# Layer 1 of a four-layer graph network: source blocks in groups of three instead of two, with VectorE's blocks at the second place of each three

## The chip, the core and the metric

The kernel runs on one core of a Trainium2 chip. The metric is device time in microseconds (us), the median of several executions. The core has five engines with a queue of their own each: TensorE (PE in the profile; its weight loads are PEld), VectorE (DVE), ScalarE (ACT), GpSimd (POOL) and SyncE (SP), which issues the DMA transfers. An engine takes its instructions in order; one that waits holds up all behind it on that engine.

## The reference, cut to what matters

Four graph layers follow each other on a dense 3327 x 3327 adjacency matrix and 64 features per node. Each ends with a residual sum and a layer norm. The change lies in layer 1:

```python
c = CURV
deg = jnp.maximum(adj.sum(axis=1, keepdims=True), 1e-08)
w = adj / deg
log_ij = _logmap(x[:, None, :], x[None, :, :], c)
agg = jnp.einsum('ij,ijc->ic', w, log_ij)
transformed = agg @ weight + bias
return _expmap(origin, transformed, c)
```

For each pair of nodes a factor that depends on the inner product of their features is multiplied with the adjacency, and the result weights a sum over the source nodes.

## The kernel before, in words

Nodes are padded to 3328: 26 blocks of 128. Destinations are taken in 4 chunks of 832 columns (two halves of 416), in the order 0, 3, 1, 2. In layer 1 (`layer1_far`, line 822) a step i is one source block of one chunk; there are 4 x 26 = 104 steps. The adjacency comes in pairs of source blocks, 832 KB each, into four buffers (`adjp`).

Each step has these parts:

- **Row products**, `far_v`, line 835: two products of 64 rows x 128 columns (one for each half), fp32, each recorded as two matmuls, so four records a block. Their result, tile `two`, takes a pair of PSUM banks; there are three such pairs, given out in rotation by `Banks.pair` (line 305). In this text V7 is the row product of step 7.
- **First factor**, line 846: VectorE reads `two` and the adjacency and writes `p` (four buffers).
- **Second factor.** A step marked "G" in `L1_ENGINES`: ScalarE squares `two` into `s` (line 859), adds a constant (line 860), and GpSimd multiplies `s` by `p` (line 861). A step marked "V": ScalarE squares `two` in place (line 851) and VectorE makes `s` from `two` and `p` (line 854, the function `last`). So `two` of a G step is free after the square, that of a V step only after line 854. The last four steps are V whatever the pattern says (`L1_LAST`).
- **Sums**, `far_aggregate`, line 866: two products of 128 rows x 64 columns with `s`, again four records a block, six steps later (`L1_AHEAD`). A7 is the sum of step 7; the accumulators are `one0` and `one1`.

The loop at line 936 takes a group of steps: first the row products of all of them, then the factors step by step, then the sums of as many steps. Within the factors, line 854 of step i-1 is issued behind the `p` of step i. TensorE's order is held by manual dependencies: row products behind the last sum of the group before (`summed`), sums behind the group's row products (`v_issued`).

```python
for start in range(0, total + L1_AHEAD, L1_GROUP):
    group = range(start, start + L1_GROUP)
    ...
    for i in group:
        ...
            v, v_issued = far_v(c, jb, summed)
    ...
    for i in group:
        ...
            s, next_last, p_issued = far_factors(v, a, engine)
        ...
        if last is not None:
            issued = last()
        ...
    for i in group:
        ...
            summed = far_aggregate(*waiting.pop(0), acc, j == 0, j == NB - 1, v_issued)
```

Other work is threaded in by step number, on the same engines: the last chunk's features from layer 0 (`features0`, line 605, from step 3 on), their transposes (`transposes0`, line 650, with copies at 656 and 657) at two steps that stand two apart, and, for every finished chunk, the copies and the product of its sums (`keep1`, lines 451 and 880), the products `own1` (line 889), and `epilogue1` with `finish1` (lines 895 and 798: products at line 903, then some 30 small VectorE operations at 910 to 923 and 804 to 820). The products of line 903 go into `pv`, which `Banks.short` takes out of the same three pairs of banks: the next one in rotation.

Of the kernel before, what the change touches and what calls it, by code (L numbers as in the profile page):

```python
# [79 lines left out]
L0_LAG = 3  # L80


L1_ENGINES = "GVGGGV"
L1_AHEAD = 6

L1_LAST = 4

L1_GROUP = 2

# [27 lines left out]
def four_gnn_layers_kernel(  # L119
# [702 lines left out]
    def layer1_far(banks):  # L822
        with tc.tile_pool(name="l1w", bufs=1) as wp:
# [19 lines left out]
            def far_factors(v, a, engine):  # L843

                p = tile_p()
                issued = nc.vector.scalar_tensor_tensor(  # L846
                    halves(p), v, 0.25 - 0.5 * FD, halves(a), op0=ALU.add, op1=ALU.mult
                )
                s = tile_s()
                if engine == "V":  # L850
                    nc.scalar.activation(v, v, AF.Square, bias=FB - 0.5, scale=-2.0)  # L851

                    def last():
                        return nc.vector.scalar_tensor_tensor(  # L854
                            halves(s), v, FG, halves(p), op0=ALU.add, op1=ALU.mult
                        )

                    return s, last, issued
                nc.scalar.activation(halves(s), v, AF.Square, bias=FB - 0.5, scale=-2.0)  # L859
                nc.scalar.activation(s, s, AF.Copy, bias=FG)  # L860
                nc.gpsimd.tensor_mul(s, s, p)  # L861
                return s, None, issued
# [72 lines left out]
            waiting, last, side, total, summed, kept = [], None, None, NCH * NB, None, {}  # L935
            for start in range(0, total + L1_AHEAD, L1_GROUP):
                group = range(start, start + L1_GROUP)
                made = []
# [11 lines left out]
                for i in group:  # L950
                    p_issued, next_last = None, None
                    if made:
                        k, jb, v, a = made.pop(0)
                        assert k == i
                        engine = L1_ENGINES[i % len(L1_ENGINES)] if i < total - L1_LAST else "V"
                        s, next_last, p_issued = far_factors(v, a, engine)
# [566 lines left out]
```

## Time and profile before

| what | us |
|---|---|
| median of 3 executions (520.52 to 521.48) | 521.14 |
| the profiled execution | 522.02 |
| its span, first to last instruction | 520.3 |
| layer 1, from the first row product to the last sum | 154.4 to 343.4 |
| PE busy over the span | 480.4 (92%) |
| DVE, ACT, POOL busy over the span | 386.2, 328.6, 179.5 |
| PE, DVE, ACT, POOL busy within 200 to 240 | 38.87, 33.37, 33.37, 31.04 |
| mean granted TensorE clock | 0.991 |

A duration is that of one instruction; a bracket behind a row tells how long its engine had stood idle and who released it. Matmul ends are modelled; starts are recorded, so distances between starts are what counts on TensorE.

### The profile page before, as it was taken

Reading aid. Unit: us, or ns where it says so; the run is one execution under the profiler, and the core shown is the slowest. Engines: PE = TensorE matmul, PEld = TensorE weight load, DVE = VectorE, ACT = ScalarE, POOL = GpSimd, SP = SyncE. Lnnn points to the kernel's source line nnn. Section 1 sums busy time; section 2 is a strip of 40 time slices with the busy share of each in tenths; the row PEclk is TensorE's granted clock in tenths of the full one; section 3 lists DMA queues with packets and bytes.
Section 4 is the critical chain, followed back from the end, with each engine's and each line's share of the span. In section 5 each row is a group of like instructions: output and inputs, shape, how many; then the busy total and the mean of one; then the engine's idle time right before and its main releaser. Section 6 shows DMA issues by size and latency. Waiting matters only on the chain. (4 is left out here: it accounts for less than half of the span.)

```text
span 520.3 us, 8496 instructions
## 1 busy us (share of the span) xinstructions
PE 480.4 (92%) x3256; PEld 240.1 (46%) x3256; DVE 386.2 (74%) x703; ACT 328.6 (63%) x395; POOL 179.5 (35%) x150
## 2 busy tenths in 40 slices
PE   5999998999967999999999899899999999999993
PEld 3554443454432333433443344354565655556662
DVE  3565438989669978789789978978689766727744
ACT  1435544776878899868977896720277943338941
POOL 2000201203018788867877695600312012200000
PEclk9999999999999999999999999989999999999997
DMA  8999999989529687767866787499869889950002
GB/s 272 321 361 345 356 395 387 332 273 322 197 85 366 224 258 274 253 198 231 289 213 205 256 260 251 148 342 370 278 214 370 289 279 367 344 188 1 1 18 56
DMA packets 46212, 132.52 MB, mean 255 GB/s; under 512 B 6967, under 2 KB 7071, under 8 KB 46099
## 3 DMA queue, kind: packets, MB, share of 16 engines
q1 hardware_dynamic: 45634, 131.35, 73.2%
q0 software_dynamic: 384, 0.52, 0.4%
q8 instruction: 27, 0.44, 0.3%
q14 instruction: 23, 0.18, 0.1%
q10 hardware_dynamic: 144, 0.03, 0.0%
HBM read 130.86 MB, written 0.85 MB: 253 GB/s over the span
## 5 line engine op out<-in xcount | busy, mean ns | idle before, releaser
L861 POOL TENSOR_TENSOR s<-s,p 128x832 f32<-128x832 f32 x67 | 130.1, 1956 | 42.0 <-ACT s L860 26.6
L846 DVE SCALAR_TENSOR_TENSOR p<-two,adj 128x832 f32<-128x832 f32 x100 | 101.2, 1019 | 18.2 <-issue 12.9
L835 PE MATMUL two<-uw 64*128 64x416 f32 x416 | 88.5, 537 | 12.9 <-DVE s L854 6.0
L549 ACT ACTIVATE rank<-two,last_bias 128x832 uint8<-128x832 f32 x78 | 71.7, 952 | 44.8 <-PE two L539 22.9
L467 PE MATMUL one<-adj,x0w 128*64 128x416 f32 x416 | 82.5, 524 | 3.7 <-DMA adj<-in_adjt_dram 2.2
L866 PE MATMUL one<-s,xu 128*64 128x416 f32 x416 | 85.2, 524 | 0.0
L859 ACT ACTIVATE s<-two 128x832 f32<-128x832 f32 x67 | 57.6, 860 | 27.2 <-DVE p L846 24.6
L525 DVE SCALAR_TENSOR_TENSOR mask<-two,minus_last,mask 32x832 bf16<-32x832 f32 x48 | 52.5, 1093 | 29.7 <-PE two L539 26.0
L835 PEld LDWEIGHTS two<-uw 64*128 64x128 f32 x416 | 37.3, 185 | 64.1 <-PE one L866 20.7
L493 DVE TENSOR_SCALAR mask<-adj 128x1664 bf16<-128x1664 f32 x48 | 51.3, 1068 | 15.8 <-DMA adj<-in_adjt_dram 15.2
L1333 PE MATMUL two<-bits,parts 128*64 128x416 bf16 x624 | 62.3, 340 | 0.0
L860 ACT ACTIVATE s<-s 128x832 f32<-128x832 f32 x67 | 60.1, 897 | 1.9
L539 PE MATMUL two<-mask,tri 128*64 128x416 bf16 x416 | 52.6, 342 | 8.7 <-DVE mask L525 6.2
L467 PE MATMUL one<-adj,xr 128*64 128x416 f32 x264 | 57.0, 514 | 0.2 <-DMA adj<-in_adjt_dram 0.2
L1333 PEld LDWEIGHTS <-parts 128*64 128x64 bf16 x624 | 36.9, 110 | 24.1 <-issue 7.3
L866 PEld LDWEIGHTS one<-s,xu 128*64 128x64 f32 x416 | 25.9, 136 | 47.5 <-issue 46.5
L467 PEld LDWEIGHTS one<-adj,x0w 128*64 128x64 f32 x416 | 29.3, 138 | 35.7 <-issue 23.6
L539 PEld LDWEIGHTS <-tri 128*64 128x64 bf16 x416 | 25.6, 110 | 41.3 <-issue 23.2
L1303 ACT ACTIVATE bits<-rank 128x1664 uint16<-128x1664 uint8 x22 | 33.6, 1580 | 14.5 <-PE two L1333 14.1
L854 DVE SCALAR_TENSOR_TENSOR s<-two,p 128x832 f32<-128x832 f32 x37 | 37.5, 1015 | 1.3 <-ACT two L851 1.3
L851 ACT ACTIVATE two<-two 128x832 f32<-128x832 f32 x37 | 31.3, 847 | 5.6 <-DVE p L846 4.8
L549 ACT ACTIVATE uw<-two,last_bias 128x832 uint8<-128x832 f32 x26 | 24.2, 950 | 12.5 <-DVE mask L525 6.4
(270 smaller groups left out, 472.3 us busy)
## 6 DMA issues: line engine op xcount, KB each, us to landing
adj<-in_adjt_dram SPq DMA_DIRECT2D x135, 832.0 KB, 5.3
uw<-in_adjt_dram SPq DMA_DIRECT2D x7, 832.0 KB, 7.3
a<-in_adjt_dram SPq DMA_DIRECT2D x8, 416.0 KB, 6.2
sums<-in_adjt_dram SPq DMA_DIRECT2D x2, 832.0 KB, 6.0
p<-in_adjt_dram SPq DMA_DIRECT2D x4, 416.0 KB, 5.3
s<-in_adjt_dram SPq DMA_DIRECT2D x4, 416.0 KB, 7.6
uw<-in_xt_dram SPq DMA_DIRECT2D x1, 640.0 KB, 10.8
out_dram<-o SPq DMA_DIRECT2D x3, 192.0 KB, 2.5
```

The lines of the kernel that those rows point to most:

```text
L467: issued = nc.tensor.matmul(acc[h * D : (h + 1) * D, 0:HC], lhsT=x[:, 2 * jp + k, 0:D], rhs=a[:, bass.ts(h, HC)], start=(first and k == 1) ...
L493: issued = nc.vector.tensor_scalar(mask, a2, 0.0, None, op0=ALU.not_equal)
L525: ranks.carried = nc.vector.scalar_tensor_tensor(halves(last), ranks.after[P - 32 : P, :, 0:HC], minus_last[P - 32 : P, :], halves(last), ...
L539: issued = nc.tensor.matmul(counts[k][rows, h, 0:HC], lhsT=lhsT[:, rows], rhs=mask[:, of, bass.ts(h, HC)], start=lhsT is tri, stop=(k == 1 ...
L549: ranks.made = nc.scalar.activation(halves(ranks.rank[:, 2 * jp + k, :]), counts[k][:, :, 0:HC], AF.Relu, bias=last_bias,)
L835: issued = nc.tensor.matmul(v[:, h, 0:HC], lhsT=wt[rows, bass.ts(jb, P)], rhs=ut[rows, bass.ds(c * CH + h * HC, HC)], start=True, stop=True,)
L846: issued = nc.vector.scalar_tensor_tensor(halves(p), v, 0.25 - 0.5 * FD, halves(a), op0=ALU.add, op1=ALU.mult)
L859: nc.scalar.activation(halves(s), v, AF.Square, bias=FB - 0.5, scale=-2.0)
L860: nc.scalar.activation(s, s, AF.Copy, bias=FG)
L861: nc.gpsimd.tensor_mul(s, s, p)
L866: issued = nc.tensor.matmul(acc[h * D : (h + 1) * D, 0:HC], lhsT=xu[:, jb, 0:D], rhs=s[:, bass.ts(h, HC)], start=first, stop=last,)
L1333: issued = nc.tensor.matmul(acc3[c][h * D : (h + 1) * D, 0:HC], lhsT=parts[:, 2 * jp + b, bass.ts(part, D)], rhs=bits[:, b, bass.ts(h, HC) ...
```

## The change

Two constants of layer 1's loop differ.

```diff
-L1_ENGINES = "GVGGGV"
+L1_ENGINES = "GVGGVG"
 L1_AHEAD = 6
 
 L1_LAST = 4
 
-L1_GROUP = 2
+L1_GROUP = 3
```

TensorE now runs three blocks' row products and then three blocks' sums. In each group of three the second step is the V step; before, V steps stood at places 1 and 5 of every six, always the second of a pair. The number of V steps stays 37 and that of G steps 67. The three pairs of banks for `two`, the four buffers of `p` and the nine of `s` are as they were. Nothing outside layer 1 is changed.

In the built order, a typical group reads on TensorE: row products of steps i, i+1, i+2, sums of i-6, i-5, i-4; on VectorE: `p` of i, i+1, i+2, then line 854 of i+1; on ScalarE: square and constant of i, square of i+1, square and constant of i+2. The two batches of transposes (4 and 3 of them), which had two groups of their own, stand in one group, and the second waits for ScalarE's copy of the first. SyncE's order of transfers is the same.

## The prediction

> **What bounds the kernel now.** First the page's chain by line, and layer 1's waits: which engine sets its pace.
>
> ```profile
> PE 34%; DVE 6%; DMA 1%; issue 0%; ACT 0%; POOL 0%; ACTq 0%
> ```
>
> ```profile
> ACT s L859 <- DVE p L846: 24.6, 31, 3.0
> ...
> PE two L835 <- DVE s L854: 6.0, 13, 0.9
> ```
> (The second block's columns: who waited for whom, us in total, times, longest.)
>
> I read it as: TensorE carries the end, and within layer 1 it is held up, once it runs, mainly where VectorE's line 854 gives a pair of banks back late. The first row says that ScalarE's square starts behind VectorE's `p` of the same block, though both only read `two`.
>
> Next TensorE's own timeline in an undisturbed stretch (start, us, engine, line, ..., records).
>
> ```profile
> 200.19 1.67 PE L835 MATMUL two<-uw 64*128 64x416 f32 x8
> 201.79 1.62 PE L866 MATMUL one<-s,xu 128*64 128x416 f32 x8
> 203.34 1.67 PE L835 MATMUL two<-uw 64*128 64x416 f32 x8
> 204.93 1.62 PE L866 MATMUL one<-s,xu 128*64 128x416 f32 x8
> ```
>
> A phase of two blocks' row products takes 1.60 us to the start of the sums, the sums 1.55 to the next row products: 3.15 for two blocks. In narrow windows the pairs of records inside a phase start 0.35 apart (202.19, 202.54, 202.89). Four pairs are 1.40, so the two changes of form cost 0.20 and 0.15, **0.35 a group**. Nine groups from 181.18 to 209.74 took 28.56, 3.173 each: almost that floor.
>
> Last, how a block's banks come free, in the full timeline:
>
> ```profile
> 204.41 1.02 DVE L846 SCALAR_TENSOR_TENSOR p<-two,adj 128x832 f32<-128x832 f32 x1 [1.20 <-issue]
> 204.45 0.85 ACT L851 ACTIVATE two<-two 128x832 f32<-128x832 f32 x1
> 205.35 1.01 DVE L854 SCALAR_TENSOR_TENSOR s<-two,p 128x832 f32<-128x832 f32 x1
> 205.47 0.86 ACT L859 ACTIVATE s<-two 128x832 f32<-128x832 f32 x1 [0.17 <-DVE p L846]
> 206.28 1.02 DVE L846 SCALAR_TENSOR_TENSOR p<-two,adj 128x832 f32<-128x832 f32 x1
> 206.36 0.90 ACT L860 ACTIVATE s<-s 128x832 f32<-128x832 f32 x1
> ```
>
> ```profile
> 228.56 1.01 DVE L854 SCALAR_TENSOR_TENSOR s<-two,p 128x832 f32<-128x832 f32 x1
> 229.72 1.67 PE L835 MATMUL two<-uw 64*128 64x416 f32 x8 [0.42 <-DVE s L854]
> ```
>
> Steps between starts: row product to `p` 1.07 (203.34 to 204.41); `p` to its square 1.06 (204.41 to 205.47); square to constant 0.89 (205.47 to 206.36); constant to the next square 0.80 (203.65 to 204.45); in-place square to line 854 0.87 (207.69 to 208.56); line 854 to a `p` behind it 0.93; line 854 to the row product that waited for its banks 1.16 (228.56 to 229.72).
>
> **The change, part by part.**
>
> *Fewer changes of form.* 104 blocks are 52 groups before and 35 after: 17 x 0.35 = 6.0 us less. The floor of a group of three is 12 x 0.35 + 0.35 = 4.55, against 4.73 for three blocks before. This is a saving only where TensorE does not wait.
>
> *All three pairs of banks are taken at once.* Before, a V block's banks were wanted again two groups later: it stands second in its group, its successor first two groups on, 6.30 - 0.78 = 5.5 us after its own start (0.78 is the distance to a group's second block: 200.19 to 200.97). Line 854 stands there behind the next group's first `p`, at 3.15 + 1.07 + 0.93 = 5.15, and the banks are back at 6.31: just in time, hence the 13 short waits. After, its successor is the second of the very next group. Follow one group from the start of its first row product (0): `p` 1.07, square 2.13, constant 3.02, in-place square of the second block 3.82 (its `p` has ended by 3.1, so ScalarE's order decides), line 854 at 4.69, the next group's second row product at **5.85**. TensorE would be there at 4.55 + 0.78 = 5.33. So the change adds a wait of up to 0.52. Behind the waiting instruction stand, on TensorE, the second and third row products and three sums, nothing else can be drawn ahead.
>
> The wait is not paid in full in each group, since the next group's first row product was issued ahead of it and starts the next chain early. From a second row product that waited to the next group's first are 3.85 (0.35 x 10 + 0.35). First to second to first again: 5.85 + 3.85 = 9.70 for two groups, **4.85 a group**, 0.30 over the floor. The other banks don't bind: the first block's are free at 2.13 + 0.86 = 2.99, the third's at about 5.6, wanted at 6.0. VectorE needs 4 x 0.94 = 3.8 and ScalarE 4.2 of the 4.85; GpSimd 3.9.
>
> 35 x 0.30 = 10.5 us added, 6.0 removed: **+4.5 us**. Against the measured 3.173 of two blocks the quiet groups alone lose 4.85 - 4.76 = 0.09 each.
>
> Bounds of the 0.30: below, nothing, if the square could run beside `p` or VectorE is ahead; above 0.52, if the first row product is never early. I take 0.30, as every step in it has a row above.
>
> A rule that speaks for the change, and one against: the Trainium skill, TensorEngine Tiling (Array Packing), section Key Properties, says that a change of tiling mode drains TensorE; the rows' 0.35 agree, and by that alone it would be 6.0 us faster. The same page, PSUM Bottleneck, says that tiling doesn't speed up the emptying of PSUM, which may become the limit; by that the 6.0 would not come at all. The trace has both, so I follow the chain of rows.
>
> *Disturbed groups.* Here I walked the built order of each engine with the steps above. Small VectorE operations cost 0.2 (0.07 alone between big ones), wide ones 0.45 to 0.5.
>
> - Start. Steps 3 to 14 carry layer 0's last features on VectorE. The page's stall there now is the fill (157.64 to 164.71). After, three groups of row products stand ahead of the first sum. Both walks are level when 12 blocks and 6 sums are done (173.8 before, 173.7 after). Then V13 waits for line 854 of step 10, which stands behind five small and two wide operations: 176.45 instead of 174.5. The second batch of transposes, now in the same group as the first, waits about 0.9 for the copy of line 657. Before had 15 blocks and 9 sums at about 179.6, after at 182.5: +2.9, of which 0.6 is in the plain sum: **+2.3**.
> - First epilogue (steps 36 to 60): `pv` of line 903 takes the banks of the group's first block and is read until line 916, which stands behind the next group's first `p`. From V36: V39 6.85, `p` 7.92, line 916 at 9.73, V40 only at 10.45, V42 at 12.5, V43 at 15.45 (it waits for line 854 of V40's block), and further V48 23.85, V54 35.25, V60 45.7. Before: 213.68 to 256.76, 43.1. +2.6, of which 1.0 is in the plain sum: **+1.6**.
> - Second epilogue (63 to 87): here line 910 stands ahead of line 854, and `pv` is read in time. 43.3 against 42.9 before, +0.4; copies of 0.5 each on ScalarE 0.4 more: +0.8, **-0.2** against the plain sum. VectorE's extra work stalls TensorE in both versions.
> - Where products of lines 889 and 903 lie between row products and sums (up to 0.92 and 1.5), the chain runs beside them and the 0.30 is hidden: steps 60 to 63 **-1.2**, steps 84 to the last sum **-2.2** (from V90 30.7 against 31.5).
>
> The five last bold numbers make +0.3; with +4.5 it is **+4.8**. The last 8 sums and what follows are as long as before (6.6 us from the last row product on), so nothing is given back behind layer 1.
>
> *Places of V steps.* V at each second place instead of one and five of six: GpSimd gets two G blocks in 4.85 and never three in a row. Its four waits of VectorE (`p` for a free buffer) are 3.8 us in all, one of them in the fill; the gain lies between 0 and 3.8. I take 0: TensorE's own waits name line 854 and the square, not `p`'s buffers. Transfers: a pair lands in 5.3 us (median) and is asked for some 11 us ahead; three blocks at once cost nothing as long as that holds, and up to one landing, 5.3, if not. I take 0.
>
> From the profiled execution, 522.0, this gives 526.8; the profiled one lies 0.9 above the median, so against the median of 521.1: **525.9 us**.
>
> **Rivals.**
>
> *TensorE sets the pace (faster).* One mechanism: if the way from the first row product to the next group's second is 5.33 or less instead of 5.85, no banks are waited for and 6.0 is gained: 515.1. For it: 92% busy TensorE, and only 6.0 us of waits on line 854 now. Against: six rows in series, all measured, would have to lose 0.52. It decides from 5.33 downward; from 5.85 to about 5.4 gain and loss cancel.
>
> *They cancel.* Half the waits are hidden by own products and epilogues: 521 within 0.2% (1.0 us), which is about what a measurement can tell from no change.
>
> *The full wait in each group.* The first row product isn't early either, since VectorE's side work delays its `p`: 35 x 0.52 = 18.2 - 6.0 = +12.2, 533.3. For it: three epilogues and the start cover some 65 of 104 steps, and VectorE is there nearly full (19.27 of 20 us from 280 to 300). Against: in the walk each second such group is without a wait.
>
> *The order isn't what the diff says.* In three groups the second row product is put behind half of the third, or behind sums; that touches 3 of 35 groups, at most 1 us, and is in the walk.
>
> **How the numbers follow.** The forecast (522.2 to 530): 0.59, 525.9. TensorE's pace (514 to 520.1): 0.19, 515.1. Cancelled: 0.12, 521. Full wait (530 to 534): 0.10, 533.3. So faster 0.19, same 0.12, slower 0.69. The range from 517 leaves out about half of the faster case, and to 532 half of the full wait: 517 to 532.
>
> **What would show it.** Row products of a group starting 4.55 and 5.1 apart in turn, or 4.85 each, in quiet stretches; a row "two L835 <- DVE s L854" of some 10 us or more instead of 6.0; line 854 at 4.7 behind its group's start; a gap ahead of V40 near line 916; the transposes' second batch waiting for line 657. It is wrong if groups start 4.55 apart without waits on line 854, if the square starts ahead of the end of its block's `p`, or if VectorE waits for transfers.

## The result and the profile after

The changed kernel is slower: 528.25 us (525.62 to 529.92, six executions) against 521.44 (520.52 to 524.3, six), a ratio of 1.0119 with an interval of 1.0082 to 1.0155; the medians differ by +6.8 us. The forecast was 525.9, in a range of 517 to 532. The profiled execution of the changed kernel took 529.92 (span 528.1), that of the kernel before 522.02 (span 520.3).

First the page's chain by engine and by line, of the kernel after.

```profile
PE 56%; DVE 25%; ACT 8%; DMA 4%; issue 3%; POOL 0%; DVEq 0%; ACTq 0%
PE one L467 16%; PE two L1333 10%; PE two L835 8%; DVE p L846 7%; PE one L866 7%; PE two L539 5%; DVE mask L525 5%; DMA adj<-in_adjt_dram 4%; PE two L467 3%; DVE s L854 3%; DVE mask L493 3%; ACT s L859 2%; ACT rank L549 2%; ACT s L860 2%; ACT two L851 1%
```

The chain of before adds up to 41% only, so the shares aren't compared; what counts is the second row. Row products (835), `p` (846), the square (859), the constant (860), the in-place square (851) and line 854 are all on it: the six steps of which the prediction built its 5.85 us.

Layer 1's waits in the kernel after (who for whom, us in total, times, longest):

```profile
ACT s L859 <- DVE p L846: 32.2, 33, 3.2
...
PE two L835 <- DVE s L854: 6.6, 9, 2.2
```

The second row was to be "some 10 us or more" and is 6.6, barely above the 6.0 of before. Read alone it would deny the mechanism. TensorE's timeline in a quiet stretch, steps 21 to 29, shows otherwise (start, us, line, records, bracket: idle time and releaser):

```profile
197.34 2.39 PE L835 MATMUL two<-uw 64*128 64x416 f32 x12
...
201.90 0.97 PE L835 MATMUL two<-uw 64*128 64x416 f32 x4
203.23 1.67 PE L835 MATMUL two<-uw 64*128 64x416 f32 x8 [0.36 <-DVE s L854]
...
207.08 2.39 PE L835 MATMUL two<-uw 64*128 64x416 f32 x12
```

Groups start 4.56 and 5.18 apart in turn, and in the second kind the second row product stands off from the first (x4, then x8) and names line 854. That wait stands in every other group only; in the rest TensorE is on time, because the group before was held. And line 854 itself, in the full timeline of the same groups:

```profile
200.38 0.90 ACT L860 ACTIVATE s<-s 128x832 f32<-128x832 f32 x1
201.18 0.85 ACT L851 ACTIVATE two<-two 128x832 f32<-128x832 f32 x1
202.06 1.02 DVE L854 SCALAR_TENSOR_TENSOR s<-two,p 128x832 f32<-128x832 f32 x1 [0.75 <-ACT two L851]
```

It starts 4.72 behind its group's first row product at 197.34 (forecast 4.69), and 203.23 - 202.06 = 1.17 later the banks are back.

Where the time of layer 1 went, from the starts of the row products on TensorE (us; V60 is the row product of step 60; "forecast" is the prediction's own working for the stretch, with the 0.13 a group of its plain sum; the last stretch is what is left of its +4.8):

| stretch | before | after | loss | forecast |
|---|---|---|---|---|
| V0 to V18, layer 0's last features | 29.90 | 35.30 | **+5.4** | +2.9 (to V15) |
| V18 to V36, undisturbed | 29.35 | 30.27 | +0.9 | +0.9 (from V15) |
| V36 to V60, first epilogue | 43.08 | 45.30 | +2.2 | +2.6 |
| V60 to the last sum's start | 86.16 | 84.61 | -1.6 | -1.6 |
| layer 1 | 188.49 | 195.48 | +7.0 | +4.8 |

In the profiled pair the first row product comes 2.4 later, at the end of layer 0, whose code is the same, and what follows layer 1 is 1.6 shorter; so the spans differ by 7.8.

The start is the one stretch that misses clearly. TensorE there, in the kernel after:

```profile
177.13 0.97 PE L835 MATMUL two<-uw 64*128 64x416 f32 x4
180.27 2.18 PE L835 MATMUL two<-uw 64*128 64x416 f32 x8 [2.17 <-DVE s L854]
182.38 1.11 PE L650 MATMUL one<-ident,twice 128*128 128x128 f32 x4
183.42 2.93 PE L866 MATMUL one<-s,xu 128*64 128x416 f32 x10
186.28 0.55 PE L650 MATMUL one<-ident,twice 128*128 128x128 f32 x3
186.76 0.91 PE L866 MATMUL one<-s,xu 128*64 128x416 f32 x2
```

V13 waits 2.17 for line 854. Then eight records take 2.18 instead of the 1.67 of other groups, and four transposes 1.11 where before had 0.66:

```profile
173.82 1.67 PE L835 MATMUL two<-uw 64*128 64x416 f32 x8
175.42 0.66 PE L650 MATMUL one<-ident,twice 128*128 128x128 f32 x4
176.01 1.62 PE L866 MATMUL one<-s,xu 128*64 128x416 f32 x8
```

The windows of the kernel after say why (bounds, length, busy us of PE, PEld, DVE, ACT, POOL with instructions, then the granted TensorE clock, DMA share, GB/s):

```profile
174.48:177.90 3.42, 3.42 (x20) 1.07 (x16) 3.39 (x6) 1.96 (x3) 2.61 (x3) 1.00 0.63 198
177.90:181.31 3.41, 1.24 (x8) 0.78 (x8) 3.16 (x5) 2.63 (x4) 2.02 (x2) 1.00 0.55 150
181.31:184.72 3.41, 3.41 (x12) 1.24 (x10) 3.24 (x4) 3.38 (x5) 3.41 (x2) 0.50 0.82 271
184.72:188.14 3.42, 3.42 (x17) 1.30 (x15) 0.99 (x2) 1.64 (x3) 2.14 (x2) 1.00 0.43 173
```

The clock is halved for 3.41 us just behind the stall. In this stretch the kernel before has full clock throughout (1.00 from 154.4 to 179.6; 0.88 in the kernel after from 156.8 to 187.6, with a first halved part from 154.0 to 160.8). That first part lies on the first row products and needs no groups of three: the run with the start in pairs, below, has it too. V6 came 8.38 us behind V0 in the kernel after, 8.41 in that run and 7.30 in the profiled execution of before. So some 1.1 of the +5.4 depends on which execution was profiled; against that run the start of the change loses 4.3.

### The profile page after: what moved, and what is told of

Same layout as the page of the kernel before. It is cut to its first block, busy times and chain, and to the rows that moved or that the text cites. A ratio compares the mean times of both kernels' runs of the same rounds, so it can differ in the third digit from the quotient of the medians.

```text
span 528.1 us, 8499 instructions
## 1 busy us (share of the span) xinstructions
PE 481.4 (91%) x3256; PEld 242.7 (46%) x3256; DVE 386.7 (73%) x703; ACT 327.6 (62%) x395; POOL 180.7 (34%) x150
## 4 chain that ended last, share of the span: by engine, by line
PE 56%; DVE 25%; ACT 8%; DMA 4%; issue 3%; POOL 0%; DVEq 0%; ACTq 0%
PE one L467 16%; PE two L1333 10%; PE two L835 8%; DVE p L846 7%; PE one L866 7%; PE two L539 5%; DVE mask L525 5%; DMA adj<-in_adjt_dram 4%; PE two L467 3%; DVE s L854 3%; DVE mask L493 3%; ACT s L859 2%; ACT rank L549 2%; ACT s L860 2%; ACT two L851 1%
## 5 line engine op out<-in xcount | busy, mean ns | idle before, releaser
L846 DVE SCALAR_TENSOR_TENSOR p<-two,adj 128x832 f32<-128x832 f32 x100 | 99.6, 1018 | 13.9 <-PE two L835 12.3
L835 PE MATMUL two<-uw 64*128 64x416 f32 x416 | 90.6, 549 | 16.4 <-DVE s L854 6.6
L866 PE MATMUL one<-s,xu 128*64 128x416 f32 x416 | 82.3, 524 | 0.0
L859 ACT ACTIVATE s<-two 128x832 f32<-128x832 f32 x67 | 57.5, 858 | 32.9 <-DVE p L846 32.2
L835 PEld LDWEIGHTS two<-uw 64*128 64x128 f32 x416 | 38.6, 189 | 66.9 <-issue 17.1
L866 PEld LDWEIGHTS one<-s,xu 128*64 128x64 f32 x416 | 27.4, 137 | 46.2 <-issue 42.4
L539 PEld LDWEIGHTS <-tri 128*64 128x64 bf16 x416 | 25.8, 110 | 41.4 <-issue 23.4
```

Source lines behind the costliest of these rows:

```text
L539: issued = nc.tensor.matmul(counts[k][rows, h, 0:HC], lhsT=lhsT[:, rows], rhs=mask[:, of, bass.ts(h, HC)], start=lhsT is tri, stop=(k == 1 ...
L835: issued = nc.tensor.matmul(v[:, h, 0:HC], lhsT=wt[rows, bass.ts(jb, P)], rhs=ut[rows, bass.ds(c * CH + h * HC, HC)], start=True, stop=True,)
L846: issued = nc.vector.scalar_tensor_tensor(halves(p), v, 0.25 - 0.5 * FD, halves(a), op0=ALU.add, op1=ALU.mult)
L866: issued = nc.tensor.matmul(acc[h * D : (h + 1) * D, 0:HC], lhsT=xu[:, jb, 0:D], rhs=s[:, bass.ts(h, HC)], start=first, stop=last,)
```

## The experiments

The theory: all three pairs of banks are taken by one group, so a group's second row product needs the banks that line 854 of the group before gives back, 5.85 us after that group began. The rivals: that the place of the V step, or the size of the group, costs by itself; that another wait (GpSimd, `p`'s buffers, transposes) sets the pace; and that the loss lies not in the quiet groups but where other work is threaded in. The tables' method (starts of row products) is used throughout.

### The V step first in each three

```diff
-L1_ENGINES = "GVGGVG"
+L1_ENGINES = "VGG"
```

> Groups of three as in the changed kernel, but VectorE finishes the first step of each three (pattern VGG). Theory (the V step's banks come back too late for the next group's product at the same place): with the V step first its way is row product to p 1.07, p to square 1.06, square to line 854 0.87, line 854 to the product that reuses the banks 1.16, in all 4.16, and wanted after 4.55; the second step's banks are back at 4.1 (wanted 5.33), the third's at 6.0 (wanted 6.03). So no waits in quiet groups, which start 4.55 apart each instead of 4.56 and 5.18 in turn, and the whole saving of 6.0 us shows: about 516 us, 513 to 520. Rival (taking all three pairs of banks at once stalls TensorE wherever the V step is): groups alternate as before, 526 us or more. Rival (the changes of form on TensorE cost nothing that can be saved): 521 us, quiet groups 4.73 apart.

Measured: 528.99 us (526.63 to 532.74, six), ratio 1.0154 (1.0111 to 1.0196). TensorE in a quiet stretch:

```profile
191.82 2.39 PE L835 MATMUL two<-uw 64*128 64x416 f32 x12
...
196.38 2.39 PE L835 MATMUL two<-uw 64*128 64x416 f32 x12
...
200.95 1.32 PE L835 MATMUL two<-uw 64*128 64x416 f32 x6
```

Groups start 4.56 and 4.57 apart, no row product waits: the floor of 4.55, as the theory says. But the total is no better: V0 to V18 takes 32.64 (+2.7 on before), V36 to V60 46.15 (+3.1), V60 to V90 56.91 (+1.8). What the quiet groups win is lost in the start and the epilogues. The expected 516 failed there. The total is that of the first rival, but the quiet groups are not: they don't alternate.

### The V step third

```diff
-L1_ENGINES = "GVGGVG"
+L1_ENGINES = "GGV"
```

> Groups of three with the V step at the third place (pattern GGV). Theory: line 854 of the third step is issued behind the next group's first p (4.55 + 1.07 + 0.94 = 6.56), its banks are back at 7.72 and wanted at 4.55 + 1.48 = 6.03; from there to the group after are 3.15, so two groups take 10.87, starting 4.55 and 6.3 apart in turn: 35 x (5.43 - 4.55) = 31 us more than the floor, 6 saved, about 546 us (540 to 552). Rival (the place of the V step does not matter, the three pairs of banks do): 526 to 530 us.

Measured: 578.98 us in one execution.

```profile
196.76 1.67 PE L835 MATMUL two<-uw 64*128 64x416 f32 x8
199.88 0.97 PE L835 MATMUL two<-uw 64*128 64x416 f32 x4 [1.45 <-DVE s L854]
...
203.02 1.67 PE L835 MATMUL two<-uw 64*128 64x416 f32 x8
206.14 0.97 PE L835 MATMUL two<-uw 64*128 64x416 f32 x4 [1.45 <-DVE s L854]
```

Each group waits 1.45 and starts 6.26 behind the one before: the later a group's V step, the longer its banks are held, and here no group recovers. The direction is the theory's; the size was underestimated: 546 was expected, with a wait in every second group only.

### Groups of three, the V steps where they were

```diff
-L1_ENGINES = "GVGGVG"
+L1_ENGINES = "GVGGGV"
```

> Groups of three with the V steps where they were before (GVGGGV: second place in one group, third in the next); the half of the change that concerns the places is undone. Theory: every second group waits as with the V step third, so two groups take about 10.87 us as well: about 545 us (538 to 551). Rival (the changed places themselves cost time, by GpSimd or by VectorE's order): faster than the changed kernel, 521 to 526 us.

Measured: 548.82 us in one execution. In quiet stretches two groups take 10.86, with this wait in every second group, the one whose predecessor ends in a V step:

```profile
202.26 1.67 PE L835 MATMUL two<-uw 64*128 64x416 f32 x8
205.44 0.97 PE L835 MATMUL two<-uw 64*128 64x416 f32 x4 [1.51 <-DVE s L854]
```

Size 3 with the old places is far worse than the change. So the change's second edit repairs most of what its first breaks.

### Groups of two, the V steps at the new places

```diff
-L1_GROUP = 3
+L1_GROUP = 2
```

> Groups of two as before, with only the places of the V steps changed (GVGGVG). Theory: the V step at place 4 is first of its pair, its banks are back 4.2 to 4.4 after its start and wanted after 3.93, so up to 0.46 in one group of three is lost, 17 times, 0 to 8 us, about half of it: 525 us (521 to 529). The loss of the changed kernel is then not in the places but in the groups of three with them. Rival (the loss of the changed kernel comes from the places alone): 528 us.

Measured: 529.64 us (526.31 to 531.03, four), ratio 1.0157 (1.0111 to 1.0204).

```profile
196.74 0.97 PE L835 MATMUL two<-uw 64*128 64x416 f32 x4
198.17 0.97 PE L835 MATMUL two<-uw 64*128 64x416 f32 x4 [0.46 <-DVE s L854]
```

Six quiet steps take 10.15 against 9.50 before, with this wait once in six: steps 1 and 4 of six put one V step first in its pair, where its banks are wanted soonest. The expected 525 (521 to 529) was too low: each wait delays its group by 0.65, not by up to 0.46. The total alone would fit the rival, 528; but per six quiet steps the places cost 0.65 in pairs and the change 0.25, so the change's loss isn't simply that of the places. Neither edit is free alone, and their costs don't add: place and size belong together.

### ScalarE squares the V step's banks earlier

After the change, ScalarE does square and constant of a group's first block, and only then the in-place square on which line 854 waits. Here the constant (and GpSimd's multiply behind it) is put behind that square.

```diff
-nc.scalar.activation(v, v, AF.Square, bias=FB - 0.5, scale=-2.0)
+squared = nc.scalar.activation(v, v, AF.Square, bias=FB - 0.5, scale=-2.0)
+if held:
+    held.pop()(squared)
...
-nc.scalar.activation(s, s, AF.Copy, bias=FG)
-nc.gpsimd.tensor_mul(s, s, p)
+def rest(behind=None):
+    added = nc.scalar.activation(s, s, AF.Copy, bias=FG)
+    if behind is not None:
+        issue_after(added, behind)
+    nc.gpsimd.tensor_mul(s, s, p)
+if later:
+    held.append(rest)
+else:
+    rest()
...
```

`later` is set for the first block of a group.

> The changed kernel with one thing moved: ScalarE squares the second (V) step of each three ahead of adding the constant to the first. Theory (the V step's banks come back at the end of a chain in which ScalarE's constant stands): the constant's 0.89 drops out of the chain except for 0.1, line 854 starts at 3.94 behind the group's start instead of 4.69, the banks are back at 5.1 and wanted at 5.33, so quiet groups start 4.55 apart without waits; from step 18 to 36 about 29.4 us less 1.2 = 28.5 instead of 30.3. The start and the epilogues stay slower than before, so about 524 us (521 to 528). Rival (the wait is for VectorE, or for something not in this chain): quiet groups 4.56 and 5.18 apart in turn as in the changed kernel, 528 us.

Measured: 529.83 us (526.31 to 531.79, six), ratio 1.0115 (1.0071 to 1.0159): the expected 524 failed, nothing was won. Lines of this kernel are shifted: 848 is `p`, 853 the in-place square, 858 the old 854, 869 GpSimd's multiply.

```profile
199.18 3.88 POOL L869 TENSOR_TENSOR s<-s,p 128x832 f32<-128x832 f32 x2 [0.90 <-ACT s L866]
...
201.17 1.96 DVE L848 SCALAR_TENSOR_TENSOR p<-two,adj 128x832 f32<-128x832 f32 x2 [0.49 <-PE two L835]
...
202.22 0.85 ACT L853 ACTIVATE two<-two 128x832 f32<-128x832 f32 x1 [0.66 <-DVE p L848]
...
203.11 1.02 DVE L858 SCALAR_TENSOR_TENSOR s<-two,p 128x832 f32<-128x832 f32 x1
203.35 2.60 PE L835 MATMUL two<-uw 64*128 64x416 f32 x12
```

Quiet groups now start 4.77 apart (198.58, 203.35), with 0.14 of wait left in each. `p` of a second block starts at 201.17; the profile names TensorE, whose row product had begun at 199.50 and is ready 1.07 later, so it isn't that. What ends just ahead is GpSimd's first multiply, half of the 3.88 behind 199.18, at some 201.12; it reads the buffer of `p` that this step takes next (there are four). The instruction at 201.17 does wait for GpSimd's semaphore, and that semaphore's last update ahead of it stands at 201.14. The shorter way to line 854 was replaced by the longer hold of `p`. A fifth buffer of `p` wasn't tried. Overall, V18 to V36 takes 30.10 (after 30.27), V36 to V60 44.57 (45.30) and V60 to V90 56.77 (54.63): what the middle wins is lost again behind V60, and why was not looked into.

### Without epilogues: pairs, V second, V first

Three kernels leave out the products `own1` and the epilogues of the first three chunks, so that layer 1 has nothing threaded in behind step 18.

```diff
-if n > 0 and OWN1_AT <= j + 1 < OWN1_AT + 4:
+if False:
...
-side = epilogue1(ORDER[n - 1], own, None)
-step(side, v_issued)
+side = None
```

> The kernel before without the own products (line 889) and the epilogues of the first three chunks in layer 1, which are left out. Theory: every six steps from 36 to 96 take 9.5 us as in the quiet stretch: about 506 us. It is the base for the next two.

> The changed kernel with the same parts left out. Theory: every six steps take 9.75, 0.25 more than in pairs, and the start is some 5 us longer: about 515 us, 8 to 9 over the run in pairs. Rival (groups of three lose in the epilogues): level with the run in pairs from step 18 on.

> Groups of three with the V step first, with the same parts left out. Theory: every six steps take 9.13, the floor, from step 18 on; 13 times 0.37 less than in pairs, with 2.8 more at the start: about 504 us, 2 under the run in pairs. Rival (the epilogues are not what eats the saving): 7 over the run in pairs, as with the epilogues.

Measured, one execution each: pairs (as before) 507.0 us, V second (as after) 516.78, V first 503.7. Six quiet steps take 9.51, 9.75 and 9.13, each as expected to 0.01. The V-first groups from the third kernel, the same over and over:

```profile
224.70 2.39 PE L835 MATMUL two<-uw 64*128 64x416 f32 x12
...
229.27 2.39 PE L835 MATMUL two<-uw 64*128 64x416 f32 x12
```

By starts, the change without epilogues loses 4.8 in V0 to V18 (36.10 against 31.26; the clock was halved there for three pieces of 3.41 us against one, so chance has a part in it) and 1.9 in all the rest of layer 1 (144.69 against 142.77). With the epilogues the rest lost 2.2 + 0.9 - 1.6 = 1.5, so in these single executions the epilogues add nothing to the change's loss overall. V first loses 1.3 at the start and wins 4.1 behind it. So groups of three with the V step first do save changes of form where nothing is threaded in; with the epilogues in place, that saving is gone.

### The start in pairs

The kernel after, but steps 0 to 17 in pairs with the old places.

```diff
-for start in range(0, total + L1_AHEAD, L1_GROUP):
-    group = range(start, start + L1_GROUP)
+threes, groups = ((18, 200),), []
+while not groups or groups[-1].stop < total + L1_AHEAD:
+    at = groups[-1].stop if groups else 0
+    size = 3 if any(a <= at < b for a, b in threes) else 2
+    groups.append(range(at, at + size))
+for group in groups:
...
+if len(group) == 3 and i < total - L1_LAST:
+    engine = "GVG"[i % 3]
```

> The changed kernel, but steps 0 to 17 go in pairs with the old places; from step 18 on groups of three with the V step second. Theory (the start is the largest loss: three groups of row products stand ahead of the first sum, the V step's banks wait behind layer 0's small operations, both batches of transposes fall into one group, and TensorE idles long enough for its clock to be halved): steps 0 to 18 take 29.9 us as before instead of 35.3, what follows is unchanged: 523 us (521 to 525). Rival (the start's loss is chance, of the halved clock in one profile): steps 0 to 18 of both within 1 us of each other in the median's sense, 527 to 528 us.

Measured: 524.66 us (523.36 to 525.71, twelve), ratio 1.0044 (1.0024 to 1.0065). V0 to V18 takes 30.98 (after 35.30; before 29.90, without the halved clock that both others have on their first row products), every stretch from V24 on is as after to 0.02, and the granted clock is 1.00 from 162 on. The start is thus the largest part of the loss: layer 1 is 195.48 - 192.34 = 3.1 shorter, the medians differ by 3.6. One thing is given back, V18 to V24 takes 10.89 instead of 9.76:

```profile
185.60 1.67 PE L835 MATMUL two<-uw 64*128 64x416 f32 x8
188.81 0.97 PE L835 MATMUL two<-uw 64*128 64x416 f32 x4 [1.54 <-DVE s L854]
```

The last pair ends in a V step, and the group of three behind it wants those banks at once.

### The second transposes three steps later

```diff
-if late is None and i in (late_at, late_at + 2):
+if late is None and i in (late_at, late_at + 3):
```

> The changed kernel with the second batch of transposes put three steps later, into the next group. Theory: the wait for the copy of the first batch (0.9 us by the forecast, more at the halved clock) goes, steps 12 to 18 take 13 to 14 us instead of 15.0, the wait for line 854 of step 10 stays (2 us): 526 to 528 us in one run. Rival (the transposes cost nothing): 15.0 for these steps.

Measured: 527.25 us in one execution. V12 to V18 takes 14.19 instead of 15.01, the 2.18 wait of V13 on line 854 stands unchanged, and so does a halved clock behind it. Two batches in one group are worth some 0.8, the wait isn't theirs. Where most of the 0.8 goes stands in the weight loads of the kernel after:

```profile
184.79 0.14 PEld L866 LDWEIGHTS one<-s,xu 128*64 128x64 f32 x2 [0.38 <-issue]
185.14 0.14 PEld L866 LDWEIGHTS one<-s,xu 128*64 128x64 f32 x1 [0.21 <-issue]
185.49 0.14 PEld L866 LDWEIGHTS one<-s,xu 128*64 128x64 f32 x1 [0.21 <-issue]
186.28 0.31 PEld L650 LDWEIGHTS one<-ident,twice 128*128 128x128 f32 x3 [0.65 <-ACT s L860]
```

In an undisturbed phase the records of sums start two at a time, each pair 0.35 behind the one before. Here the second batch stands between the two products of one step, and that step's four records start singly (185.49 and 185.84 ahead of it, 186.76 and 187.16 behind it): two places of 0.35 more, 0.7 in all. In this run all twelve start in pairs.

### Threes only where they win

V-first threes at steps 18 to 35, 54 to 59 and 66 to 71, pairs elsewhere.

```diff
+threes, groups = ((18, 36), (54, 60), (66, 72)), []
...
+if len(group) == 3 and i < total - L1_LAST:
+    engine = "VGG"[i % 3]
```

> Groups of three with the V step first only where VectorE has no side work (steps 18 to 36, 54 to 60, 66 to 72), pairs with the old places elsewhere. Theory: the first stretch gains 0.8 us, the two others 0.2 and 0.5 against pairs: 519.5 to 520.5 us where the kernel before has 521.5, about the least that can be told. Rival (each change from pairs to threes costs a wait of its own): 521.5 or more.

Measured: 524.15 us (522.16 to 526.64, twelve), ratio 1.0027 (0.9999 to 1.0055). V24 to V30 is 9.08, as it should be, but the six steps behind each change from pairs to threes take 10.89, 11.22 and 10.91, with a wait on line 854 like the one above. The rival (each change of size costs a wait) holds in the trace; the expected 519.5 to 520.5 was missed, and the total can't be told from the kernel before, as the interval holds 1. No version of the whole kernel that was tried beats the kernel before.

## Why the prediction was right, and where it was off

- **Form changes and the chain of banks: right, and shown.** The floor of 4.55 is met where nothing waits (4.56), the groups of the change come 4.56 and 5.18 apart (forecast 4.55 and 5.15), 4.87 in the mean (4.85), line 854 at 4.72 (4.69). Moving the V step to the first place takes the wait away, to the third makes it 1.45. The rival in which TensorE sets the pace is out, and so is the full wait in each group.
- **The start: right in sign, mis-sized.** "After at 182.5: +2.9" was +5.4 to V18. Counted from the first row product, 12 blocks and 6 sums were forecast to be done at 19.3 and were at 20.3, V13 came at 23.4 instead of 22.0, and 9 sums were done at 30.8 instead of 28.1. Of the 2.7, 1.0 was there when 12 blocks and 6 sums were done. The run with the start in pairs tells what that most likely is: with a like halved clock on its first row products it is 1.1 behind before at V6 and still so at V18. So this part isn't the change's. Another 0.4 came with V13's wait. The other 1.3 lies behind V13, where the clock was 0.50. By starts, the eight records took 2.11 (1.60 in before), the four transposes 1.04 (0.59) and the first two pairs of records of sums 1.37 (0.75), some 1.6 more; the sums that start singly add 0.7; and the 0.9 that the forecast had put there for line 657 did not come. The prediction took every duration at full clock and had no term for a stall that slows what follows it, nor for sums that no longer start in pairs. That the clock adds those 1.6 is read from the rows; that it would not have been halved without the stall wasn't tried.
- **The second transposes' wait for line 657: wrong.** In the trace ten records of sums stand between the two batches; line 657 ended at 185.00 and the second batch started at 186.28, behind sums. The 0.9 of the prediction didn't come; in its place the batch parted a step's sums, at 0.7.
- **First epilogue: right.** V40 stands 10.5 behind V36 (forecast 10.45) and waits, as forecast, for line 916 with `pv` in its banks:

```profile
232.21 0.56 DVE L916 SCALAR_TENSOR_TENSOR one<-z,two 128x384 f32<-128x384 f32 x1
...
232.92 0.97 PE L835 MATMUL two<-uw 64*128 64x416 f32 x4 [0.51 <-DVE one L916]
```

- **Second epilogue and the end: right.** V63 to V87 took 43.05 (43.3), V90 to the end of the last sum 30.5 (30.7). V60 to V84 is 0.4 shorter than before (0.3 is left for it in the forecast) and V84 to the last sum 1.2 (1.3).
- **GpSimd and transfers at nothing: right for this kernel.** No wait of `p` for a transfer is among layer 1's large ones. The version with the earlier square shows that GpSimd's hold on `p` lies only a little behind the bound that was found.
- **The sum.** 4.8 was forecast, 6.8 measured between the medians, 7.0 in layer 1 of the profiled pair. The start's 2.5 in excess and the first epilogue's -0.4 give nearly all of the 2.2 between 7.0 and 4.8; without the 1.1 of the first halved clock layer 1 would have lost 5.9. The executions of the changed kernel spread over 4.3 us; the profiled one, at 529.92, had a mean clock of 0.985, the one at 525.62 had 0.991, as the profiled execution of before (522.02). The order isn't strict: 528.01 had 0.981.
- **A slip among the rivals.** "From 5.85 to about 5.4 gain and loss cancel" doesn't follow from the prediction's own sum: with a way of W a group takes (W + 3.85) / 2, and 35 such groups lose just the 6.0 that is saved at W = 5.59.
- **The expected row "10 us or more": wrong.** In every other quiet group the wait is 0.36, not 0.52, as the row counts from the end of the record before, and other waits of a weight load stand under PEld. Distances between starts carried the proof; the row of waits didn't.

## What to carry to other kernels

When steps are grouped to save a fixed cost, count the buffers that one group takes: as soon as it takes all of them, the buffer freed last within a group decides, and its place in the group is worth more than the saving (4.56, 4.87 or 6.26 a group for the first, second or third place). A quiet loop's gain can be measured by itself by leaving the threaded work out, and should then be tried with it in, since here it was eaten there. And a stall of TensorE of about 2 us may cost more than itself: here some 1.6 us more, through the halved clock behind it.

## What the runs showed of the hardware

The granted TensorE clock is halved in pieces of 3.41 us, on a fixed grid within an execution: in the kernel after from 154.0 to 160.8 and from 181.3 to 184.7, with 6 x 3.41 between them. Over the grids of eight of these executions, from 60 us on and up to the work's end, each piece in which TensorE was busy for 1.50 us or less was followed by a piece at half clock (ten of ten), from 1.5 to 2.4 both happened, and four pieces with 3.4 us busy were followed by one too, three of them between 343 and 354 with over 3 us of weight loads; for those the profile shows no reason. So whether a stall of 2 us halves the clock may depend on where the grid cuts it.

What it costs shows in the first six steps of layer 1, V0 to V6, which four of the kernels run in the same pairs: 7.30 us in the profiled execution of before, without a halved piece, 8.41 with the start in pairs, 8.55 in pairs without epilogues and 9.50 with threes only where they win, with the clock halved for 5.7, 3.1 and 6.1 us of it. Steps 6 to 18 differ by 0.2 at most. That the 4 us by which whole executions of one kernel spread have the same cause is argued, not shown.

The Trainium skill, TensorE: Matmul & The Clock Gate, Part 1, states a free-running window of 3413 ns, which the rows agree with, and half rate after an idle window of that length; here 1.24 us of work in the window didn't keep the clock up, so by the trace the window need not be idle.

In the kernel after, ScalarE's square of line 859 waits for VectorE's `p` of the same block 33 times, 32.2 us in all, though both only read `two`. The Trainium skill, PSUM — Partial Sum Buffer, Terms, counts two engines' reads of one bank at once among the collisions; the order in the traces, square behind the end of `p` in all 104 steps before and after, agrees with it.
